# Depthwise taps of 20 middle rows moved to VectorE in a fused conv, attention and FFN kernel

## The chip, the cores and the metric

The kernel runs on one core of a Trainium2 chip. The metric is the device time of one launch in microseconds; 64 images go through in one launch.

## The reference

Two layers on x of shape (64, 96, 56, 56), cut to what matters here:

```python
# layer 0: expand, shift, shuffle, depthwise 3x3, gate, project, residual
out = silu(bn(einsum('bchw,oc->bohw', x, expand_w)))          # 96 -> 192 channels
out = channel_shuffle(shift_groups(out), groups=4)
dw  = bn(conv3x3_depthwise(out, dw_w))                        # 192 channels, padding 1
out = silu(bn(dw + bn(out * id_w)))
se  = relu(grouped_1x1(mean(out, (2, 3)), se_red_w, se_red_b))
se  = sigmoid(grouped_1x1(se, se_exp_w, se_exp_b))
x   = silu(bn(einsum('bchw,oc->bohw', out * se, proj_w)) + x)
# layer 1 on tokens t (b, 3136, 96)
h = relu(bn(layernorm(t) @ w1.T))                             # 192 wide
X = fft(h, axis=1);  y = ifft(relu(X.real*r - X.imag*i + rb) + 1j*relu(X.imag*r + X.real*i + ib)).real
t = t + bn(y @ w2.T)
t = t + q(q(relu(q(q8(layernorm(t)) @ q8(W1).T + b1))) @ q8(W2).T + b2)   # fp8 (e5m2) products
```

## The kernel before

Each image passes through a chain of small steps, each a Python function on one engine. `STEPS` lists them; `PLAN` gives each step instance a planned time, and the loop at the end issues the steps of all 64 images in the order of `b * PERIOD + PLAN[step][i]`. The numbers are used for nothing else: they only set the order in which each engine's queue gets its instructions, so that several images overlap. An engine works its queue in that order. Names end in what they do: `_mm` on TensorE; `ea_ev`, `eb_ev`, `dw_ev`, `ls`, `se1_ev`, `se2_th`, `pj_ev`, `c_sq`, `n_sq`, `sp_ev`, `f1_ev`, `f2_u`, `f2_r`, `w2_ev`, `i1_ev`, `x_ev`, `h_ev`, `h_q`, `o_ev` on ScalarE; `lt`, `se2_ev`, `se2_pw`, `pj_add`, `c_v`, `n_v`, `sp_v`, `w1_ev`, `f2_s`, `f2_p`, `i2_ev`, `n_x`, `h_b`, `o_b` on VectorE; `c_pow`, `n_pow`, `o_f` on GpSimd (POOL); the loads `x_in` and stores `o_st` on SyncE's (SP) queue.

The chain of one image: `ea` and `eb` expand (128 channels into `e_a`, L383; the other 64, in two half images, into `e_b`, L400). `dw` (L446) computes the 3x3 taps of the first 128 channels on TensorE as 32x32 diagonal matmuls, 16 tiles at a time, in two passes of 28 rows (4 strips of `PJ` = 7 rows, 392 columns each); `dw_ev` (L456) applies SiLU and sums for the gate. `lt` (L466, L468) computes the 9 taps of the other 64 channels on VectorE, one multiply and eight multiply-adds on 128 x 1568; `ls` (L471) is their SiLU. `se1`, `se2` compute the gate, `se2_pw` folds it into the projection weights, `pj` (L532, L537) projects, `pj_add` adds x and `pj_ev` (L549) writes the tokens. `c` and `sp` are the first layer norm, `w1` (L626, L638), `f1` (L653, L665), `f2` (L680, L690, L705 to L734), `w2` (L745, L757), `i1` (L786) and `i2` (L808) the spectral layer, `n` and `x` the second layer norm, `h` and `o` the FFN.

PSUM has two pools. `psa` is two double banks used in turn by `w1`, `f1`, `f2`, `w2`, `i1`, `i2`: each of these matmul steps waits until the user before last is read out (for `f2` by `f2_u` and `f2_s`). `psb` is four single banks for everything else; a `dw` pass and a `pj` half take all four at once. Every fp32 matmul appears in the trace as two instructions with a weight load each.

The set-up ahead of the loop loads the weights and tables, folds the batch norms on VectorE, and computes one product on TensorE (`ps_w1c`, L300), which stands ahead of all steps in TensorE's queue.

Of the kernel before, what the change touches and what calls it, by code (L numbers as in the profile page):

```python
# [7 lines left out]
F32 = mybir.dt.float32  # L8
# [3 lines left out]
ALU = mybir.AluOpType  # L12
# [17 lines left out]
PJ = 7  # L30
NG = 5
# [10 lines left out]
PERIOD = 116.056  # L42
PLAN = {
    "x_in": (-142.751, -132.334, -138.890, -139.641, -151.208, -133.652, -137.370),
    "ea_mm": (-127.116, -124.446, -119.920, -94.498, -104.745, -112.167, -106.964),
    "ea_ev": (-125.252, -124.279, -119.721, -94.105, -94.974, -110.456, -105.960),
    "eb_mm": (-110.852, -109.364, -102.468, -94.672, -100.705),
    "eb_ev": (-109.889, -108.508, -98.175, -94.671, -100.704),
    "dw_mm": (-77.186, -75.415, -71.686, -59.708, -58.836, -58.630),
    "dw_ev": (-67.184, -68.088, -65.354, -62.005, -53.949, -53.481, -53.376, -53.432),  # L50
    "lt": (-93.236, -91.843, -90.397, -86.333, -83.176, -78.618, -75.060, -71.072, -58.358),
    "ls": (-56.957,),
    "se1_mm": (-52.674,),
    "se1_ev": (-52.590,),
    "se2_mm": (-49.560,),
    "se2_ev": (-47.764,),
    "se2_th": (-46.882,),
    "se2_pw": (-44.842,),
    "pj_mm": (-44.604, -44.263, -36.259, -33.499),
    "pj_add": (-41.623, -41.337, -40.573, -40.255, -32.468, -30.814, -32.509, -32.127),  # L60
    "pj_ev": (-41.036, -40.637, -40.429, -36.736, -30.334, -29.230, -31.146, -29.797),
    "c_mm": (-24.403, -20.404, -19.123, -17.297, -18.726, -9.644, -8.872),
    "c_sq": (-23.198, -19.663, -17.391, -16.366, -11.963, -8.651, -8.871),
    "c_v": (-21.831, -17.939, -17.390, -11.021, -10.842, -8.366, -8.657),
    "c_pow": (-19.058, -12.292, -10.931, -8.952, -1.526, -3.948, -1.526),
    "sp_v": (-8.951, -1.525),
    "sp_mm": (-6.057, 0.802),
    "sp_ev": (-5.461, 1.113),
    "w1_mm": (1.423, -2.619, 3.588, 18.203, 8.943, 12.171, 13.999, 16.535),
    "w1_ev": (3.273, -0.045, 7.600, 20.920, 11.591, 14.999, 15.957, 19.212),  # L70
    "f1_mm": (21.608, 26.248, 24.638, 31.810, 32.559, 32.004),
    "f1_ev": (25.169, 25.895, 30.841, 28.844, 27.556, 26.595, 32.009, 32.411, 36.910, 36.732, 36.699, 35.929),
    "f2_mm": (37.220, 36.994, 44.528, 54.196, 60.721, 63.959),
    "f2_u": (39.991, 41.910, 38.664, 38.665, 56.185, 56.316, 56.071, 58.643, 62.858, 62.962, 66.464, 67.055),
    "f2_s": (42.369, 43.646, 41.684, 42.524, 58.496, 59.412, 59.011, 59.603, 66.349, 66.780, 67.365, 69.133),
    "f2_r": (44.699, 46.227, 59.499, 60.966, 71.228, 72.985),
    "f2_p": (46.153, 47.154, 60.124, 60.967, 72.402, 74.345),
    "w2_mm": (70.359, 71.061, 73.352, 79.154),
    "w2_ev": (70.421, 73.788, 79.483, 82.773),
    "i1_mm": (82.811, 83.639, 91.924),  # L80
    "i1_ev": (86.931, 93.317, 99.344),
    "i2_mm": (102.107, 101.737, 110.644, 111.766),
    "i2_ev": (106.004, 107.037, 104.651, 104.395, 113.248, 110.645, 115.503, 113.393),
    "n_mm": (109.042, 108.523, 116.336, 120.505, 126.604, 126.539, 137.374),
    "n_sq": (109.105, 109.021, 116.337, 120.506, 127.174, 126.540, 137.375),
    "n_v": (109.642, 109.022, 116.338, 120.507, 127.975, 126.902, 138.122),
    "n_pow": (110.809, 110.170, 116.496, 122.658, 132.126, 129.135, 139.318),
    "n_x": (112.520, 110.693, 119.248, 123.053, 133.298, 130.929, 139.362),
    "x_mm": (113.125, 114.113, 121.321, 126.216, 135.244, 138.382, 142.002),
    "x_ev": (114.896, 115.709, 126.025, 126.217, 137.926, 142.365, 142.302),  # L90
    "h_mm": (
        144.408, 144.539, 142.955, 151.653, 146.123, 151.741, 165.593, 167.081, 167.021, 179.037, 181.701, 184.163,
        183.315, 191.401, 194.122, 202.572, 203.025, 214.978, 205.482, 214.132, 209.133,
    ),
    "h_ev": (
        146.457, 147.163, 146.728, 153.132, 153.156, 154.262, 168.465, 171.753, 169.119, 180.037, 185.733, 184.280,
        187.040, 192.972, 195.243, 203.531, 205.107, 216.376, 208.878, 222.205, 212.052,
    ),
    "h_b": (
        146.899, 148.834, 148.614, 154.505, 157.941, 159.836, 170.515, 176.287, 174.097, 185.812, 187.639, 185.918,  # L100
        191.781, 195.030, 198.861, 204.123, 206.545, 220.428, 209.152, 226.370, 218.475,
    ),
    "h_q": (
        149.384, 151.139, 150.029, 159.215, 163.340, 163.159, 172.257, 183.329, 182.397, 187.024, 188.763, 189.403,
        196.328, 198.478, 200.406, 208.755, 210.002, 221.499, 217.314, 229.791, 224.579,
    ),
    "o_mm": (153.028, 179.101, 192.712, 203.850, 207.474, 223.800, 230.382),
    "o_ev": (154.015, 179.621, 193.552, 207.958, 209.955, 223.824, 232.254),
    "o_b": (167.276, 193.254, 201.506, 209.696, 210.604, 235.187, 237.499),
    "o_f": (171.766, 199.519, 206.356, 219.602, 231.322, 259.139, 253.186),  # L110
    "o_st": (197.792, 218.616, 214.282, 229.895, 257.122, 313.688, 263.438),
# [4 lines left out]
def conv_attn_ffn(  # L116
# [30 lines left out]
    tab_sel: bass.AP,  # L147
# [21 lines left out]
    nc.sync.dma_start(out=xi[GAP : GAP + 1].rearrange("p a b -> p (a b)"), in_=tab_ones)  # L169
# [17 lines left out]
    mid = load(mid_par, [128, 2, 22], "mid")  # L187
    mid_g = load(mid_grp, [128, NG, 12], "mid_g")
# [7 lines left out]
    eye = load(tab_eye, [CP, CP], "eye")  # L196
    sel = load(tab_sel, [CP, 2, 128], "sel")
# [10 lines left out]
    l_tab = load(tab_l, [128, NK, CP], "l_tab", nc.scalar)  # L208
    inv_tab = load(tab_inv, [CP, 2, HW], "inv_tab", nc.scalar)
    r_tab = load(tab_r, [128, HW, HW], "r_tab", nc.scalar)  # L210

    eps = const.tile([128, 1], F32, name="eps")
    nc.vector.memset(eps, 1e-5)
    mhalf = const.tile([128, NJ], F32, name="mhalf")
    nc.vector.memset(mhalf, -0.5)
# [35 lines left out]
    eyes = load(tab_eyes, [128, 32], "eyes")  # L251
# [7 lines left out]

    def row_fold(src, n, rows, name):  # L260

        b = work.tile([128, 4, n], F32, tag="ue", name=name + "_p")
        nc.gpsimd.dma_start(out=b[0:rows], in_=src.rearrange("(o f) c -> o f c", o=1).to_broadcast([rows, 4, n]))
        s = work.tile([128, 2, n], F32, tag="s", name=name)
        s = s[0:rows]
        nc.scalar.activation(s[:, 0], b[0:rows, 3, :], AF.Sqrt, bias=eps[0:rows])
        nc.vector.reciprocal(s[:, 0], s[:, 0])
        nc.vector.tensor_tensor(s[:, 0], s[:, 0], b[0:rows, 0, :], ALU.mult)
        nc.vector.tensor_tensor(s[:, 1], b[0:rows, 2, :], s[:, 0], ALU.mult)
        nc.vector.tensor_tensor(s[:, 1], b[0:rows, 1, :], s[:, 1], ALU.subtract)  # L270
# [7 lines left out]
    for e in range(2):  # L280
        nc.vector.tensor_copy(
            ex_b[:, e, :, e, :], ex_w[:, 128:MID].rearrange("p (u e i) -> p u e i", u=2, e=2)[:, :, e, :]
        )
# [26 lines left out]
    nc.vector.tensor_copy(eye8, eye, saturate=False)  # L310
# [16 lines left out]

    e_a = const.tile([128, PAD, PAD], F32, name="e_a")  # L330
    nc.gpsimd.memset(e_a, 0.0)
    e_b = const.tile([128, HH + 2, PAD], F32, name="e_b")
    nc.gpsimd.memset(e_b, 0.0)
    for i in range(NT):
        nc.vector.memset(t_buf[i], 0.0)

    buf_h = const.tile([128, C * HW + 8], F32, name="buf_h")
    nc.vector.memset(buf_h, 0.0)
    h_v = buf_h[:, 0 : C * HW].rearrange("p (c b) -> p c b", b=HW)
    pq_a = buf_h[:, 0 : NK * CP].rearrange("p (k f) -> p k f", f=CP)  # L340
    pq_b = buf_h[:, NK * CP : (NK + NS) * CP].rearrange("p (k f) -> p k f", f=CP)
    p_v = buf_h[:, 0 : 48 * HW].rearrange("p (b o) -> p b o", o=48)

    buf_g = const.tile([128, NK * MID], F32, name="buf_g")
    nc.vector.memset(buf_g, 0.0)
    g_v = buf_g.rearrange("p (k c) -> p k c", c=MID)
    u_v = buf_g[0:CP, 0 : C * 32].rearrange("p (o k) -> p o k", k=32)
    rs_full = const.tile([128, 2, NJ], F32, name="rs_full")
    nc.vector.memset(rs_full, 0.0)


# [24 lines left out]
    def x_in(b, i):  # L376
        load_x(b, i)
# [726 lines left out]
```

## Time and profile before

| what | value |
|---|---|
| median of 3 runs | 7462.52 us (7462.07 to 7469.69) |
| the profiled execution's own time | 7463.64 us |
| its span (first to last instruction) | 7461.9 us |
| granted TensorE clock, mean | 0.991 |
| busy: PE, PEld, DVE, ACT, POOL | 96%, 70%, 65%, 62%, 20% |
| first matmul of an `ea` step / of `f1` | 44.2 us / 130.16 us |
| last image's first `f1` matmul | 7332.96 us |

The page gives each engine's busy time (PE is TensorE, PEld its weight loads, DVE VectorE, ACT ScalarE), the chain of waits that ended last, and groups of instructions by source line: count after the x, then busy us, mean ns of one, idle time before it and what ended that. The ends of matmuls are modelled, so PE's busy share is not its efficiency.

### The profile page before, as it was taken

To read this page: it belongs to the slowest core of one execution; us is meant where nothing else is said; L and a number is where in the kernel's file an instruction comes from. 1 tells how busy PE (TensorE), PEld (TensorE's weight loads), DVE (VectorE), ACT (ScalarE), POOL (GpSimd) and SP (SyncE) were. 2 spreads that over 40 slices of the span, in tenths; PEclk is the share of its full clock that TensorE was granted. 3 is DMA by queue.
4 is the path that set the end of the run, shared out by engine and by line. 5 is a ranking of instruction groups with operands and counts; after the bars stand their busy time and mean duration, and the time that the engine had idled before them with its cause. 6 is when DMAs were issued, how large, how long until landed. Compare 5 with 4: busy or idle time off the path is not lost.

```text
span 7461.9 us, 383252 instructions
## 1 busy us (share of the span) xinstructions
PE 7176.9 (96%) x177666; PEld 5259.2 (70%) x177666; DVE 4829.5 (65%) x8795; ACT 4654.4 (62%) x9806; POOL 1513.6 (20%) x1360
## 2 busy tenths in 40 slices
PE   7999999999999999999999999999999999999997
PEld 4777777777777776777777777777777777777775
DVE  5666666666666666666666666666666666666664
ACT  3566666666665666656656666666566566665665
POOL 0221212212212122122121221221212212212112
PEclk9999999999999999999999999999999999999998
DMA  1010110110101101101011011010110110101100
GB/s 48 20 27 18 29 27 19 29 24 21 28 17 29 27 19 28 24 22 28 17 29 27 19 28 25 22 28 18 29 27 19 29 26 20 29 21 26 28 20 21
DMA packets 424331, 185.32 MB, mean 25 GB/s; under 512 B 378785, under 2 KB 422041, under 8 KB 422473
## 3 DMA queue, kind: packets, MB, share of 16 engines
q1 hardware_dynamic: 420970, 155.82, 9.1%
q8 instruction: 1392, 22.81, 1.3%
q10 hardware_dynamic: 1264, 3.48, 0.1%
q14 instruction: 209, 1.71, 0.1%
q0 software_dynamic: 496, 1.50, 0.1%
HBM read 82.80 MB, written 77.07 MB: 21 GB/s over the span
## 4 chain that ended last, share of the span: by engine, by line
PE 85%; ACT 6%; DVE 6%; issue 3%; DMA 0%; POOL 0%; POOLq 0%; SPq 0%; ACTq 0%
PE psa L653 9%; PE psa L626 9%; PE ps_d L446 8%; PE ps_eb L400 5%; PE ps_ea L383 5%; PE psa L808 5%; PE ps_pj L532 5%; PE ps_c L557 5%; PE psa L745 5%; PE ps_n L557 5%; PE psa L786 5%; PE psa L680 4%; PE ps_h L865 4%; PE ps_o L887 3%; DVE s L721 3%
## 5 line engine op out<-in xcount | busy, mean ns | idle before, releaser
L903 POOL TENSOR_TENSOR o<-t,o 112x448 f32<-112x448 f32 x448 | 613.9, 1370 | 3694.7 <-DMA out_dram<-o 1710.0
L446 PE MATMUL ps_d<-e_a,diag 32*32 32x392 f32 x36864 | 1033.2, 498 | 0.7 <-ACT d L456 0.7
L468 DVE SCALAR_TENSOR_TENSOR d_last<-e_b,taps,d_last 128x1568 f32<-128x1568 f32 x512 | 971.5, 1898 | 7.1
L875 DVE TENSOR_SCALAR y<-y,qb 128x448 f16<-128x448 f16 x1344 | 479.8, 365 | 683.9 <-ACT y L870 676.7
L568 DVE TENSOR_REDUCE v<-sq 112x4 f32<-112x384 f32 x896 | 491.3, 548 | 662.7 <-ACT sq L564 662.1
L446 PEld LDWEIGHTS ps_d<-e_a,diag 32*32 32x32 f32 x36864 | 673.6, 103 | 288.9 <-issue 40.0
L870 ACT CAST y<-ps_h 128x448 f16<-128x448 f32 x1344 | 697.2, 540 | 213.1 <-PE ps_h L865 209.5
L837 POOL TENSOR_TENSOR rs<-v,mhalf 112x4 f32<-112x4 f32 x448 | 490.3, 1099 | 1453.9 <-DVE v L569 1453.9
L881 ACT CAST h<-y 128x448 fp8e5<-128x448 f16 x1344 | 739.0, 571 | 3.0 <-DVE y L875 3.0
L653 PEld LDWEIGHTS psa<-f_tab,buf_h 128*56 128x56 f32 x24576 | 655.4, 131 | 77.8 <-DVE v L569 42.5
L626 PEld LDWEIGHTS psa<-w1c,t 112*64 112x64 f32 x14336 | 604.0, 137 | 141.4 <-DVE v L569 45.4
L653 PE MATMUL psa<-f_tab,buf_h 128*56 128x58 f32 x24576 | 688.9, 216 | 0.0
L626 PE MATMUL psa<-w1c,t 112*64 112x96 f32 x14336 | 676.2, 249 | 2.9 <-DMA t<-dev_t 1.4
L586 POOL TENSOR_TENSOR rs<-v,mhalf 112x4 f32<-112x4 f32 x448 | 447.6, 1012 | 763.6 <-DVE v L569 763.5
L638 DVE SCALAR_TENSOR_TENSOR buf_h<-psa,rs_full 128x768 f32<-128x768 f32 (+1 forms) x512 | 435.4, 851 | 137.4 <-PE psa L626 129.5
L543 DVE TENSOR_TENSOR ps_pj<-ps_pj,x 112x392 f32<-112x392 f32 x512 | 260.6, 566 | 404.5 <-PE ps_pj L537 392.3
L728 ACT ACTIVATE s<-s 128x896 f32<-128x896 f32 (+2 forms) x384 | 334.4, 887 | 288.8 <-DVE s L721 288.8
L388 ACT ACTIVATE e_a<-ps_ea 128x448 f32<-128x448 f32 x448 | 244.9, 547 | 412.5 <-PE ps_ea L383 412.5
L564 ACT ACTIVATE sq<-ps_n 112x384 f32<-112x384 f32 x448 | 214.1, 495 | 436.1 <-PE ps_n L557 434.8
L734 DVE SCALAR_TENSOR_TENSOR buf_h<-ue,s 128x448 f32<-128x448 f32 (+2 forms) x768 | 406.8, 580 | 109.4 <-ACT s L728 109.4
L549 ACT ACTIVATE t<-ps_pj,pjbn_b 112x392 f32<-112x392 f32 x512 | 281.4, 620 | 284.5 <-DVE ps_pj L543 284.5
L786 PE MATMUL psa<-inv_tab,buf_g 112*32 112x56 f32 x24576 | 350.5, 214 | 110.5 <-issue 108.8
(175 smaller groups left out, 13024.5 us busy)
## 6 DMA issues: line engine op xcount, KB each, us to landing
x<-in_x SPq DMA_DIRECT2D x896, 84.0 KB, 3.2
out_dram<-o SPq DMA_DIRECT2D x896, 84.0 KB, 2.2
l_tab<-in_tab_l ACTq DMA_DIRECT2D x1, 1624.0 KB
r_tab<-in_tab_r ACTq DMA_DIRECT2D x1, 1568.0 KB
t<-dev_t SPq DMA_DIRECT2D x64, 7.0 KB, 2.1
t<-dev_t SPq DMA_DIRECT2D x64, 5.2 KB
ex_row_p<-in_expand_row POOLq DMA_DIRECT2D x1, 336.0 KB, 4.5
s_p<-in_bn POOLq DMA_DIRECT2D x1, 288.0 KB, 3.8
```

The lines of the kernel that those rows point to most:

```text
L446: nc.tensor.matmul(pss[r][j * 32 : j * 32 + 32], lhsT=diag[pr, tap, :], rhs=e_a[pr, r0 : r0 + PJ, dx : dx + HW], start=tap == 0, stop=tap ...
L468: nc.vector.scalar_tensor_tensor(d_last, win, w, d_last, ALU.mult, ALU.add)
L557: nc.tensor.matmul(cen[c0:c1, k, 0:C], lhsT=t_of(b)[:, n0 + c0 : n0 + c1], rhs=center, start=True, stop=True)
L568: nc.vector.tensor_reduce(v, sq, AX.X, ALU.add)
L626: nc.tensor.matmul(ps[hc * 64 : hc * 64 + 64, k, 0:C], lhsT=t[:, n0 : n0 + 64], rhs=w1c[:, hc * C : hc * C + C], start=True, stop=True,)
L653: nc.tensor.matmul(ps[r * 64 : r * 64 + HW, k, 0 : 2 * NK], lhsT=buf_h[:, n0 : n0 + HW], rhs=f_tab[:, r, :], start=True, stop=True,)
L786: nc.tensor.matmul(ps[p0 : p0 + 32, k, 0:HW], lhsT=u_v[:, oh * 48 + o, :], rhs=inv_tab[:, r, :], start=True, stop=True,)
L837: nc.gpsimd.tensor_tensor(rs, held.pop(("nv", b, g)), mhalf[0:CP, 0:4], ALU.pow)
L870: nc.scalar.copy(y16, held.pop(("h", b, i)))
L875: nc.vector.tensor_scalar(y16, y16, qb1[:, i % 3 : i % 3 + 1], 0.0, ALU.add, ALU.max)
L881: nc.scalar.copy(held["h8", b, j][:, m, :], held.pop(("y", b, i)), saturate=False)
L903: nc.gpsimd.tensor_tensor(o32, rows, o16, ALU.add)
```

## The change

The middle 20 rows (18 to 37) of the first 128 channels are taken from TensorE: `mt` computes their nine taps on VectorE from `e_a` into `d_mid` (128 x 1120), with `ms` as their SiLU and sum on ScalarE. The other 36 rows (9 + 9 at the top, 9 + 9 at the bottom) go through `dw` in one pass with strips of `PJ` = 9 rows, 504 columns. The projection of the middle rows is one matmul of 128 channels and 5 rows (280 columns) per strip in place of four of 32 channels. The gate has 6 sums instead of 9. `sp_mm` selects with four half-width matmuls from the identity table in place of two with `tab_sel`, which is gone. In the set-up, x of the first image is loaded right after `ex_w`, `ex_w` is folded first, `mid`, `mid_g` and `eyes` are loaded by ScalarE's queue, and `l_tab` and `r_tab` come last on SP. All times of `PLAN` and `PERIOD` are new (those of the steps named below are shown).

```diff
-PJ = 7
-NG = 5
+PJ = 9
+M0 = 2 * PJ
+MR = HW - 4 * PJ
+MJ = MR // 4
+NG = 6
-PERIOD = 116.056
+PERIOD = 140.265
...
-    "dw_mm": (-77.186, -75.415, -71.686, -59.708, -58.836, -58.630),
+    "dw_mm": (-112.745, -112.718, -112.047),
-    "lt": (-93.236, -91.843, -90.397, -86.333, -83.176, -78.618, -75.060, -71.072, -58.358),
+    "lt": (-136.700, -135.995, -135.558, -134.088, -134.025, -130.160, -122.585, -110.579, -107.986),
+    "mt": (-164.940, -164.052, -163.371, -149.054, -134.393, -134.063, -132.364, -119.142, -113.460),
+    "ms": (-111.901,),
-    "se1_mm": (-52.674,),
+    "se1_mm": (-94.074,),
-    "pj_mm": (-44.604, -44.263, -36.259, -33.499),
+    "pj_mm": (-69.552, -69.551, -65.748, -61.381),
-    "w1_ev": (3.273, -0.045, 7.600, 20.920, 11.591, 14.999, 15.957, 19.212),
+    "w1_ev": (-1.771, -19.170, -8.762, -4.229, -10.279, -4.199, -8.276, -1.831),
-    "f1_mm": (21.608, 26.248, 24.638, 31.810, 32.559, 32.004),
+    "f1_mm": (9.106, 8.289, 6.986, 1.458, 9.457, 8.749),
-    "f2_mm": (37.220, 36.994, 44.528, 54.196, 60.721, 63.959),
+    "f2_mm": (11.234, 10.157, 22.124, 26.950, 29.584, 36.004),
-    "f2_s": (42.369, 43.646, 41.684, 42.524, 58.496, 59.412, 59.011, 59.603, 66.349, 66.780, 67.365, 69.133),
+    "f2_s": (13.743, 13.743, 12.484, 12.496, 26.842, 26.842, 27.498, 31.087, 34.039, 34.367, 47.926, 51.650),
-    "w2_mm": (70.359, 71.061, 73.352, 79.154),
+    "w2_mm": (57.877, 50.003, 70.914, 73.115),
...
+    for i in range(NCH):
+        load_x(0, i)
...
     def x_in(b, i):
-        load_x(b, i)
+        if b > 0:
+            load_x(b, i)
...
-    d_buf = const.tile([128, 2, 4, PJ, HW], F32, name="d")
+    d_buf = const.tile([128, 4, PJ, HW], F32, name="d")
+    d_mid = const.tile([128, MR, HW], F32, name="d_mid")
...
+    def start_row(n):
+        i, j = divmod(n, 4)
+        if i == 0:
+            return j % 2 * (M0 + MR) + j // 2 * PJ, PJ
+        return M0 + (j % 2 * 2 + j // 2) * MJ, MJ
...
-    def dw_mm(b, n):
-        i, third = divmod(n, 3)
+    def dw_mm(b, third):
...
+    def one_tap(d, e, h, r0, n):
         tap = (4, 0, 1, 2, 3, 5, 6, 7, 8)[n]
         dy, dx = divmod(tap, 3)
+        win = e[:, r0 + dy : r0 + dy + d.shape[1], dx : dx + HW]
+        w = taps[:, h, tap : tap + 1]
         if n == 0:
+            nc.vector.tensor_scalar(d, win, w, None, ALU.mult)
         else:
+            nc.vector.scalar_tensor_tensor(d, win, w, d, ALU.mult, ALU.add)
+    def lt(b, n):
+        one_tap(d_last, e_b, 1, 0, n)
...
+    def mt(b, n):
+        one_tap(d_mid, e_a, 0, M0, n)
+    def ms(b, i):
+        nc.scalar.activation(d_mid, d_mid, AF.Silu, bias=mid_b[:, 5:6], accum_out=sums_of(b)[:, 5:6])
...
+        elif part == 0:
             for j in range(4):
+                r0, n = start_row(4 + j)
+                nc.tensor.matmul(
+                    pss[j], lhsT=pw[:, 5, :], rhs=d_mid[:, r0 - M0 : r0 - M0 + n, :], start=True, stop=False
+                )
```

Sorted, the new `PLAN` puts these steps on VectorE from one `w1_ev0` on, while TensorE has `f1` and `f2` of the same image b (the taps are those of image b + 1): `n_x4, n_x6, lt0, lt1, lt2, mt4, lt3, mt5, lt4, mt6, h_b3, lt5, h_b0, f2_s2, f2_s3, h_b4, f2_s0, f2_s1, h_b5, lt6, o_b5, mt7, h_b2, f2_p1, h_b1, f2_p0, o_b6, mt8, f2_s4, f2_s5, f2_s6, f2_p2, lt7, f2_s7, lt8, f2_p3, f2_s8, f2_s9`. `mt0` to `mt3` come before it, among `n_v`, `n_x`, `i2_ev` and `w1_ev`. TensorE's order there is `f1_mm3, 2, 1, 5, 0, 4`, `f2_mm1, f2_mm0, f2_mm2, f2_mm3, dw_mm0` to `2`, `f2_mm4, f2_mm5, se1_mm, w2_mm1, se2_mm, w2_mm0, pj_mm0`, with x, o, h and ea products between.

## The prediction

> **What bounds the kernel now.** I read the page's busy shares first, then its chain:
>
> ```profile
> PE 7176.9 (96%) x177666; PEld 5259.2 (70%) x177666; DVE 4829.5 (65%) x8795; ACT 4654.4 (62%) x9806; POOL 1513.6 (20%) x1360
> ...
> PE 85%; ACT 6%; DVE 6%; issue 3%; DMA 0%; POOL 0%; POOLq 0%; SPq 0%; ACTq 0%
> ```
>
> TensorE sets the end, VectorE and ScalarE have a third of the span free. But these are averages over stages. The groups of the work that changes:
>
> ```profile
> L446 PE MATMUL ps_d<-e_a,diag 32*32 32x392 f32 x36864 | 1033.2, 498 | 0.7 <-ACT d L456 0.7
> L468 DVE SCALAR_TENSOR_TENSOR d_last<-e_b,taps,d_last 128x1568 f32<-128x1568 f32 x512 | 971.5, 1898 | 7.1
> ```
>
> The taps of the first 128 channels cost TensorE 1033.2/64 = 16.1 us an image; the other 64 channels' taps cost VectorE 15.2 us plus one multiply of 1.04. Then I cut one image's period into stages with the windows view (from f1 of one image to f1 of the next, so two to three images are in flight in each). Columns: stretch, length, busy us of PE, PEld, DVE, ACT, POOL, clock:
>
> ```profile
> 2989.60:3028.00 38.40, 38.40 (x1144) 30.06 (x1140) 34.33 (x44) 30.06 (x63) 3.38 (x3) 1.00 0.02 4
> 3028.00:3036.50 8.50, 7.67 (x210) 6.34 (x209) 5.77 (x14) 7.34 (x18) 0.00 (x0) 1.00 0.01 4
> 3036.50:3050.10 13.60, 13.60 (x195) 8.04 (x192) 4.98 (x12) 8.91 (x18) 1.30 (x1) 1.00 0.23 53
> 3050.10:3065.40 15.30, 13.22 (x478) 10.37 (x476) 6.13 (x17) 9.85 (x19) 4.82 (x5) 0.89 0.38 84
> 3065.40:3105.00 39.60, 39.60 (x769) 27.44 (x768) 23.68 (x51) 16.41 (x40) 13.98 (x14) 1.00 0.06 16
> ```
>
> This table carries the prediction. Row 1 (f1, f2 and both `dw` passes, up to `se1_mm`) has VectorE busy 34.33 of 38.40 us: no 65% there, but 89%. Row 5 has it at 60%. Where the new taps fall decides what they cost.
>
> In the timeline, what TensorE and VectorE do back to back:
>
> ```profile
> 3005.84 7.95 PE L446 MATMUL ps_d<-e_a,diag 32*32 32x392 f32 x288
> ...
> 3050.09 2.86 PE L786 MATMUL psa<-inv_tab,buf_g 112*32 112x56 f32 x216
> 3055.03 1.00 PE L786 MATMUL psa<-inv_tab,buf_g 112*32 112x56 f32 x40 [2.08 <-issue]
> ```
> ```profile
> 3126.71 0.33 DVE L875 TENSOR_SCALAR y<-y,qb 128x448 f16<-128x448 f16 x1
> 3126.96 1.84 DVE L468 SCALAR_TENSOR_TENSOR d_last<-e_b,taps,d_last 128x1568 f32<-128x1568 f32 x1
> 3128.72 2.22 DVE L734 SCALAR_TENSOR_TENSOR buf_h<-ue,s 128x448 f32<-128x448 f32 x4
> ```
>
> One pass of 9 taps takes 7.9 us. A VectorE instruction's successor starts about 0.08 us before its end (3126.96 + 1.84 against 3128.72), so I count start to start. The first `f1` starts at 130.16 and the last at 7332.96: 63 periods of **114.33 us**. Span = 130.2 + 63 x 114.33 + 128.9 = 7461.9; the execution's own time is 7463.64, 1.7 more, and the median of the runs shown is 7462.52, 1.1 below it.
>
> **The Trainium skill.** "PSUM — Partial Sum Buffer", Specifications (TRN2): a bank holds 512 fp32 values, so 9 rows x 56 = 504 just fit; the trace has 392. "VectorE: DVE Perf Modes", Mode 1× (REGULAR): fp32 with a second tensor runs at one result a cycle, 0.96 GHz; 1568 elements are 1.63 us, the trace shows 1.84 to 1.90. "SBUF — State Buffer", Who interferes with whom: a VectorE instruction with two SBUF inputs collides with a GpSimd one that reads SBUF. The taps' median is 1.850, their mean 1.898, their maximum 2.277, which agrees. The `mt` taps are of that kind.
>
> **The change, part by part, per image.**
>
> *TensorE, taps.* 288 of 576 matmuls go; the others grow from 392 to 504 columns. A group of 16 tiles now takes 7.9/18 = 0.439 us. A long row shows what a column costs: `ea` (448 columns) and `eb` (392) spend 0.445 and 0.363 us per matmul step, at most 0.83 ns a column; so 0.439 + 112 x 0.83 = 0.532, x18 = **9.6 us** (8.0 if nothing grows, 10.2 in proportion). Two passes back to back take 15.9: 6.3 saved. What hides the new pass is below: `f2_mm4` behind it waits for `f2_s5` on VectorE anyway, so 8.0 or 10.2 instead of 9.6 moves nothing; without that cover they are worth -1.6 or +0.6.
>
> *TensorE, projection.* Columns: before 2 x (4 x 392 + 2 x 392) per row group; after 6 x 504 + (4 + 2) x 280: both 4704. The full-height matmuls of 280 columns run one at a time, those of 32 rows four at a time, which the count includes. Nothing; bounds -0.5 to +1 us.
>
> *TensorE, gate and selector.* `se1` loses 3 of 9 matmuls (x2 instructions x 34 ns = -0.2), `se2` gains one, `sp_mm` has 4 half-width matmuls for 2 (0 to +0.5). Nothing.
>
> *ScalarE.* Eight `dw_ev` of 0.78 (0.586 + 0.203 for the sum) become four of about 0.92 and one `ms` of 1.4: -1.2 us. Not the bound.
>
> *VectorE.* Added: `mt`, one multiply (1.04 x 20/28 = 0.74) and eight taps of 1120 elements. Start to start a `lt` tap takes 1.76 undisturbed and 1.82 on average; by size 1.26, by the page's cycle for the 448 elements that are missing 1.35; I take 1.30. Sum **11.1 us**. `mt0` to `mt3` lie in the last stage (row 5), under TensorE: nothing. `mt4` to `mt8` lie between `f1` and `se1`: 6.5 us in row 1's stage.
>
> *That stage after the change.* The order says what VectorE does there, in one unbroken run from `w1_ev0`, which `f1_mm3` waits for, to `f2_s9`, which frees the PSUM buffer of `w2_mm1`: nine `lt` (1.0 + 8 x 1.82 = 15.6), five `mt` (6.5), eight `f2_s` of 448 (pairs, 1.31 each: 10.5), two of 392 (1.21: 2.4), four `f2_p` (1.07: 4.3), six `h_b` and two `o_b` (0.25: 2.0), two `n_x` (0.47: 0.9). **42.2 us.** TensorE's own work there, `f1_mm3` to `f2_mm5`: 38.4 - 6.3 and some 3.5 of x, o and ea products that the new order has there, about 36. I looked for each of these VectorE steps whether its ScalarE input is there in time (`f2_u`, `f2_r`, `h_ev` in that queue's order): it is, so VectorE runs through. The stage goes from 38.4 to 42.2: it gives back the whole saving and 3.8 more. The waits that this adds: TensorE stands before `f2_mm2` and `f2_mm3` (PSUM held until `f2_s3`, `f2_s1`) with `dw` queued behind, and before `w2_mm1` with the gate behind; ScalarE's `ms` waits for `mt8`, with `f2_r2` and all `dw_ev` queued behind, and the h products wait for the banks that these free. All of it lies inside the 42.2, since VectorE meanwhile has work.
>
> *Then the gate.* `se1_mm` waits for `ls` and `o_ev0`; `w2_mm1` for `f2_s9`. ScalarE has queued in front of `h_ev12`, whose bank `pj_mm0` needs: 9.6 us of `ls`, `o_ev`, `f2_u`, `f2_r4`, four `h_q`, four `h_ev`; it gets there 7.4 us after `f2_s9` (8.5 now, row 2).
>
> *Then TensorE alone,* from `pj_mm0` to the next `w1_ev0`: rows 3 to 5 take 68.5 us now, of which my sum of single steps explains 65.1; the other 3.4 are mostly the wait of 2.08 for instructions and its clock of 0.89. The new order's steps there add up to 62.9 (the products that moved into the first stage are missing). There the `i1` steps are apart, with slower matmuls between them, so I keep a third of that wait: **64.0** (62.9 to 66.3).
>
> Period: 42.2 + 7.4 + 64.0 = **113.6**, against 114.33.
>
> *Start.* The first `ea` starts at 44.2 us, after `ps_w1c` at 43.3, which VectorE's fold of w1 releases behind memsets of 2.7 to 4.7 us each. The new order loads x and folds ex_w first, but the w1c product stays ahead in TensorE's queue: -10 us (0 to -25). Moved DMAs: SP issues x at 0.78 us each (11 in 8.56), so the constants behind them come 11 us later; l_tab and r_tab, last on SP now, are wanted after 120 us. Three small loads go to ScalarE's queue. x_in of later images stays where SP has gaps (3058 to 3074). The first image's taps take 27 us of VectorE beside 10 of TensorE, for 19 of TensorE now: the first image gives some of the start back, in the -10.
>
> Sum: 7461.9 + 63 x (113.6 - 114.33) - 10 = 7406; + 1.7 - 1.1: **7405 us**. Break-even is a period of 114.5, or a VectorE stage of 43.1.
>
> **Rivals.**
>
> *VectorE's stage is longer (slower).* If the taps and products cost their listed means without overlap (`lt` 1.90, `mt` 1.39, `f2_s` 1.37, `f2_p` 1.23), the stage is 45.5 us, the period 116.9, the time 7461.9 + 63 x 2.57 - 10 + 0.6 = **7615**. For it: collisions with POOL's sums, five more taps exposed to them. Against: start-to-start times in the timeline. It decides from 43.1 us on; any wait of TensorE on POOL's or ScalarE's short chains adds the same way.
>
> *The saving arrives whole.* TensorE stays the bound: 114.33 - 6.3 = 108.0, **7057**. Row 1's 34.33 + 6.5 speaks against it: VectorE can't fit into 32.
>
> *No difference.* Stage and waits cancel within 0.2% (about what a measurement of this kernel can tell from no change), 7448 to 7477; the shift of 0.77% is small beside the terms.
>
> *The loads first do nothing,* because ps_w1c holds TensorE: +10 on the forecast, inside its range.
>
> **How the numbers follow.** Forecast (small gain) 0.47, its own range 7240 to 7447: low end with mt at 1.26 and no wait for instructions, a period of 111. Whole saving 0.05, no difference 0.09, slower 0.39. Faster 0.52, same 0.09, slower 0.39. Both signs are likely, so the range is 7240 to 7640.
>
> **What would show it.** Right: TensorE's busy share falls to some 92 to 93%, VectorE's rises to 74%; in row 1's stage VectorE is over 95% busy and TensorE waits for VectorE's `s`, `ue` (f2_s) at f2 and w2; `dw` has one pass of about 9.6 us; `mt` taps of 1.35 listed; the stage is 41 to 43.5 us. Wrong: a stage under 39 us with TensorE full; or TensorE waiting in row 5's stage; or a first `ea` still at 44 us.

## The result and the profile after

The kernel after the change takes 7642.35 us (median of 4 runs, 7634.26 to 7651.36) beside 7465.10 us of the kernel before on the same chip (7462.07 to 7469.69): a ratio of **1.0237 (95% interval 1.0219 to 1.0255), slower by 2.4%**. The forecast was 7405 us with a range to 7640. The profiled execution has a span of 7632.3 us.

The page after: busy shares, the shares of the chain that ended last, and three groups (busy us in total, mean ns of one).

```profile
PE 6957.4 (91%) x157954; PEld 5111.4 (67%) x157954; DVE 5425.0 (71%) x9367; ACT 4640.9 (61%) x9422; POOL 1763.2 (23%) x1366
...
PE 62%; DVE 26%; issue 6%; ACT 3%; POOL 3%; DMA 0%; POOLq 0%; SPq 0%; ACTq 0%; DVEq 0%
...
L478 DVE SCALAR_TENSOR_TENSOR d_last<-e_b,taps,d_last 128x1568 f32<-128x1568 f32 x512 | 945.5, 1847 | 9.7
...
L478 DVE SCALAR_TENSOR_TENSOR d_mid<-e_a,taps,d_mid 128x1120 f32<-128x1120 f32 x512 | 705.7, 1378 | 4.6
...
L457 PE MATMUL ps_d<-e_a,diag 32*32 32x504 f32 x18432 | 617.0, 590 | 0.0
```

The operations cost what the forecast said: the one `dw` pass is 617.0/64 = 9.64 us of TensorE (16.1 before), a middle tap 1.378 us listed. VectorE's part of the chain that ended last went from 6% to 26%. Yet TensorE's busy time fell by only 219.5 us, although 6.5 us x 64 = 416 us of `dw` went. Something made its other work longer.

The period is cut as before, now for the image whose `f1` starts at 3403.80: `f1` to `se1` (VectorE's stage below), `se1` to `pj_mm0` (the gate), `pj_mm0` to the next `f1` (the last part); then four stretches around the border of the first two. Columns of the windows view: stretch, length, busy us of PE, PEld, DVE, ACT, POOL, granted TensorE clock, DMA share, GB/s.

```profile
3403.80:3445.74 41.94, 36.73 (x887) 27.40 (x887) 41.27 (x51) 31.54 (x63) 6.98 (x3) 0.98 0.06 15
3445.74:3454.98 9.24, 8.55 (x180) 7.40 (x180) 5.34 (x14) 6.88 (x16) 0.00 (x0) 0.71 0.02 4
3454.98:3521.07 66.09, 62.41 (x1406) 44.24 (x1401) 37.44 (x83) 33.85 (x71) 20.22 (x19) 1.00 0.14 32
3440.55:3443.16 2.61, 0.01 (x2) 0.00 (x0) 2.57 (x3) 1.99 (x4) 0.00 (x0) 1.00 0.00 0
3443.16:3444.32 1.16, 1.16 (x19) 0.89 (x20) 1.16 (x3) 1.11 (x2) 0.00 (x0) 1.00 0.03 7
3444.32:3451.15 6.83, 5.66 (x85) 4.55 (x79) 5.46 (x13) 5.09 (x11) 0.00 (x0) 0.50 0.01 2
3451.15:3454.98 3.83, 3.83 (x112) 3.06 (x104) 1.27 (x3) 3.21 (x8) 0.00 (x0) 1.00 0.02 4
```

Row 1 is the stage that the forecast put on VectorE: 41.27 of 41.94 us busy. Row 4 is TensorE idle for 2.61 us in it. Row 6 is new: 1.2 us after TensorE has resumed, its **granted clock falls to one half for 6.83 us**. The timeline shows what that does (start, length, idle before it and who ended it):

```profile
3439.15 1.40 PE L923 MATMUL ps_o<-h,q 128*112 128x448 fp8e5 x6
3443.16 0.35 PE L901 MATMUL ps_h<-xq,q 96*128 96x448 fp8e5 x1 [2.60 <-ACT y L906]
...
3447.07 2.82 PE L781 MATMUL psa<-w2a,buf_h 128*64 128x96 f32 x32 [0.68 <-DVE ue L760]
...
3452.72 1.53 PE L781 MATMUL psa<-w2a,buf_h 128*64 128x96 f32 x32
```

The same 32 `w2` matmuls take 2.82 us at half clock and 1.53 at full. The idle ahead of `h_mm10` waits for a PSUM bank that ScalarE's `h_ev6` frees; `h_ev6` stands behind `f2_r3`, and that waits for VectorE:

```profile
3441.17 0.95 ACT L764 ACTIVATE s<-s 128x896 f32<-128x896 f32 x1 [0.82 <-DVE s L757]
3442.02 0.66 ACT L741 ACTIVATE ue<-psa,fb 128x392 f32<-128x392 f32 x1
3442.59 0.95 ACT L906 CAST y<-ps_h 128x448 f16<-128x448 f32 x2
```

The waits view (us in total, times, longest) has three waits that the kernel before does not have in its list:

```profile
DVE d_mid L476 <- ACT e_a L396: 327.3, 63, 5.2
...
PE ps_n L586 <- DVE xt L879: 84.8, 62, 1.4
...
PE psa L662 <- DVE t L857: 37.2, 62, 0.6
```

In VectorE's timeline the first one stands where `mt0` heads the queue:

```profile
3377.08 0.56 DVE L879 TENSOR_TENSOR xt<-ps_n,rs 112x384 fp8e5<-112x384 f32 x1 [1.04 <-POOL rs L873]
3382.86 0.81 DVE L476 TENSOR_SCALAR d_mid<-e_a,taps 128x1120 f32<-128x1120 f32 x1 [5.22 <-ACT e_a L396]
3383.70 2.81 DVE L478 SCALAR_TENSOR_TENSOR d_mid<-e_a,taps,d_mid 128x1120 f32<-128x1120 f32 x2
3386.43 0.33 DVE L911 TENSOR_SCALAR y<-y,qb 128x448 f16<-128x448 f16 x1
3386.67 1.16 DVE L857 SCALAR_TENSOR_TENSOR t<-psa,bn2c_b,t 112x392 f32<-112x392 f32 x2
```

VectorE stands 5.22 us for `ea` of group 2, and then three taps run while `h_b16`, `i2_ev7`, `i2_ev6` (L857) and the norm steps wait behind them.

The means over all 63 periods, from the starts of `f1`, `se1` and `pj_mm0` and the records of the granted clock in each trace. Half clock is the time that the trace records at a granted clock of one half. All periods below are read in this way; the last of the 63 is shorter in every trace, since no further image follows.

| kernel | f1 to se1 | se1 to pj_mm0 | pj_mm0 to f1 | period | half clock per period |
|---|---|---|---|---|---|
| before | 38.56 | 8.41 | 67.36 | 114.33 | 0.92 |
| after | 41.90 | 9.48 | 65.87 | 117.25 | 8.67 |

The span adds up: first `f1` at 118.6 + 63 x 117.25 + 126.8 behind the last = 7632.

### The profile page after: what moved, and what is told of

Its sections match the earlier page's. It is cut to its first block, busy times and chain, and to the rows that moved or that the text cites. A ratio compares the mean times of both kernels' runs of the same rounds, so it can differ in the third digit from the quotient of the medians.

```text
span 7632.3 us, 343376 instructions
## 1 busy us (share of the span) xinstructions
PE 6957.4 (91%) x157954; PEld 5111.4 (67%) x157954; DVE 5425.0 (71%) x9367; ACT 4640.9 (61%) x9422; POOL 1763.2 (23%) x1366
## 4 chain that ended last, share of the span: by engine, by line
PE 62%; DVE 26%; issue 6%; ACT 3%; POOL 3%; DMA 0%; POOLq 0%; SPq 0%; ACTq 0%; DVEq 0%
PE psa L689 9%; PE psa L662 6%; PE psa L781 6%; DVE s L757 5%; PE psa L844 5%; DVE ue L760 4%; DVE d_mid L478 4%; PE psa L822 4%; PE ps_c L586 4%; PE ps_eb L408 4%; DVE buf_h L770 4%; PE ps_pj L554 3%; PE psa L793 3%; PE ps_n L586 3%; POOL rs L873 3%
## 5 line engine op out<-in xcount | busy, mean ns | idle before, releaser
L939 POOL TENSOR_TENSOR o<-t,o 112x448 f32<-112x448 f32 x448 | 834.8, 1869 | 3582.3 <-DVE o L933 2463.7
L478 DVE SCALAR_TENSOR_TENSOR d_mid<-e_a,taps,d_mid 128x1120 f32<-128x1120 f32 x512 | 705.7, 1378 | 4.6
L662 PEld LDWEIGHTS psa<-w1c,t 112*64 112x64 f32 x14336 | 611.3, 137 | 99.4 <-DVE t L857 45.5
L572 DVE TENSOR_TENSOR ps_pj<-ps_pj,x 112x504 f32<-112x504 f32 (+1 forms) x512 | 261.6, 568 | 541.6 <-PE ps_pj L566 532.6
L457 PE MATMUL ps_d<-e_a,diag 32*32 32x504 f32 x18432 | 617.0, 590 | 0.0
L716 PEld LDWEIGHTS psa<-l_tab,buf_g 128*64 128x64 f32 x7424 | 387.4, 145 | 341.4 <-issue 157.7
L901 PE MATMUL ps_h<-xq,q 96*128 96x448 fp8e5 x1344 | 474.1, 377 | 152.4 <-ACT y L906 138.5
L895 ACT CAST xq<-ps_x 96x448 fp8e5<-96x448 f32 x448 | 236.0, 527 | 557.0 <-PE ps_x L888 557.0
L716 PE MATMUL psa<-l_tab,buf_g 128*64 128x112 f32 x7424 | 446.6, 275 | 114.8 <-DVE ue L760 113.2
L578 ACT ACTIVATE t<-ps_pj,pjbn_b 112x504 f32<-112x504 f32 (+1 forms) x512 | 279.6, 625 | 373.2 <-DVE ps_pj L572 364.6
L457 PEld LDWEIGHTS ps_d<-e_a,diag 32*32 32x32 f32 x18432 | 370.0, 103 | 199.6 <-issue 53.4
```

Of the source, the lines that this page charges most:

```text
L457: nc.tensor.matmul(pss[r][j * 32 : j * 32 + 32], lhsT=diag[pr, tap, :], rhs=e_a[pr, r0 : r0 + PJ, dx : dx + HW], start=tap == 0, stop=tap ...
L478: nc.vector.scalar_tensor_tensor(d, win, w, d, ALU.mult, ALU.add)
L662: nc.tensor.matmul(ps[hc * 64 : hc * 64 + 64, k, 0:C], lhsT=t[:, n0 : n0 + 64], rhs=w1c[:, hc * C : hc * C + C], start=True, stop=True,)
L716: nc.tensor.matmul(ps[c0 : c0 + 64, k, 0:CP], lhsT=g_v[:, k1, c0 : c0 + 64], rhs=l_tab[:, k1, :], start=True, stop=True,)
L939: nc.gpsimd.tensor_tensor(o32, rows, o16, ALU.add)
```

## The experiments

Theory 1 at the start: the gain was lost to the clock, which halves after the idle that VectorE's long stage leaves on TensorE. Its rivals: the gate has its own chain and the clock is a symptom; or VectorE's longer stage is the whole loss. All edits are to the kernel after the change, all ratios are to the kernel before on the same chip.

**Filling TensorE's idle.** The same sum is made five times over, so that only the idle goes.

```
-        for m in range(3):
+        for _ in range(5 if j == 0 else 1):
+            for m in range(3):
```

> The kernel after the change, with the three matmuls of o_mm of the first group made five times over (each repetition starts the sum anew, so the value is the same): 12 matmuls, some 2.6 us of TensorE work per image put into TensorE's idle stretch ahead of h_mm10; nothing else is moved. Theory 1 (the forecast lost its gain to TensorE's clock, which halves after that idle stretch and stays down for 7 to 17 us of every period): the clock stays at 1.00 through the period (half clock under 1.5 us per period, 8.7 before this edit), the VectorE-bound stage stays at 42, the gate returns to 7.4 to 8.0, the rest to 64 to 65; period about 113.5, time 7370 to 7450. Rival 1 (the gate's chain through ScalarE and VectorE sets its length and the clock is only a symptom): 7620 to 7660. Rival 2 (VectorE's longer stage is the whole loss): 7620 to 7660, and with the added TensorE work no gain anywhere.

7573.6 us, ratio 1.016 (1.0143 to 1.0177): by the two ratios some 57 us less than after, but above the 7370 to 7450 of theory 1. Period 116.19 (41.85 + 8.63 + 65.71), half clock 3.14 us. Two neighbouring periods of this trace, three rows each:

```profile
3375.65:3417.60 41.95, 38.65 (x899) 28.92 (x899) 41.29 (x51) 31.55 (x62) 7.14 (x3) 1.00 0.05 15
3417.60:3424.94 7.34, 6.31 (x180) 5.43 (x180) 5.50 (x14) 6.89 (x16) 0.00 (x0) 1.00 0.01 2
3424.94:3490.01 65.07, 62.07 (x1413) 44.06 (x1405) 37.40 (x82) 33.96 (x72) 20.13 (x19) 1.00 0.14 32
3490.01:3531.96 41.95, 38.49 (x899) 28.94 (x899) 41.29 (x51) 31.55 (x62) 7.13 (x3) 1.00 0.06 15
3531.96:3540.76 8.80, 7.77 (x179) 6.78 (x180) 5.50 (x14) 6.89 (x16) 0.00 (x0) 0.81 0.02 5
3540.76:3606.37 65.61, 62.03 (x1413) 44.15 (x1405) 37.41 (x82) 33.86 (x72) 20.13 (x19) 1.00 0.14 32
```

One kernel, one order: with the clock kept the gate is 7.34, the forecast's 7.4; with half clock in it 8.80. In the 22 of 63 periods without half clock the gate is 7.34 every time, and the parts are 41.94 + 7.34 + 65.75 = 115.03; in the 32 with 3.4 us of it the gate is 8.6 to 8.9. So the clock is real, but it is not all: the last part stays at 65.7, where the forecast had 64.0.

**One order on ScalarE.** `f2_r[3]` goes behind `h_ev6`, `h_ev7` and `f2_u9` (31.088 to 31.373).

> The kernel after the change, with f2_r[3] moved on ScalarE behind h_ev6, h_ev7 and f2_u9, so that h_mm10's bank comes free without waiting for VectorE's f2_s7. Theory 1 (an idle stretch of TensorE anywhere in the VectorE-bound stage halves the clock; the stage has some 36 us of TensorE work in 42): the idle stretch of 2.6 us ahead of h_mm10 goes and stands later instead, ahead of h_mm9, se1 or w2_mm1; the clock still halves for 7 us or more per period, time 7590 to 7650. Rival (that one order on ScalarE is the cause): no long idle, clock 1.00, 7390 to 7480.

7648.34 us, 1.0259 (1.0244 to 1.0275): no gain, as theory 1 said. TensorE's idle went elsewhere:

```profile
3566.18 0.64 PE L497 MATMUL ps_se<-sums,rd_w 128*24 128x1 f32 x12 [2.43 <-ACT o L928]
3567.50 2.82 PE L781 MATMUL psa<-w2a,buf_h 128*64 128x96 f32 x32 [0.68 <-DVE ue L760]
```

Now 2.43 us ahead of `se1`, and again `w2` at 2.82. The half clock is 6.72 us per period. A wait moved inside a stage that another engine sets only moves the idle.

**The taps out of VectorE's stage**, without and with the filling:

```
-    "ea_mm": (-166.379, -168.555, -167.472, -180.658, -173.715, -159.950, -127.809),
-    "ea_ev": (-164.984, -167.775, -166.091, -178.609, -172.105, -156.666, -124.805),
+    "ea_mm": (-166.379, -167.472, -168.555, -180.658, -173.715, -159.950, -127.809),
+    "ea_ev": (-164.984, -166.091, -167.775, -178.609, -172.105, -156.666, -124.805),
-    "mt": (-164.940, -164.052, -163.371, -149.054, -134.393, -134.063, -132.364, -119.142, -113.460),
+    "mt": (-165.930, -165.830, -164.930, -164.830, -164.530, -164.030, -158.930, -149.050, -148.530),
```

> The kernel after the change, with the middle rows' taps out of the VectorE-bound stage: ea_mm and ea_ev of groups 1 and 2 change places, mt0 to mt5 stand one after the other where VectorE waited 5.2 us for e_a, mt6 to mt8 among the w1_ev of the last stage; VectorE's work between f1 and f2_s9 falls by five taps of 1.30, from 42.0 to about 35.5. Theory 1: that stage becomes TensorE's own, 36.5 to 38.5; no idle over 1 us is left in it, the clock stays at 1.00 (half clock under 2 us per period), gate 7.4 to 8.5, the rest 64 to 66.5; period 109 to 112, time 7110 to 7300. Rival 1 (the gate's length comes from its ScalarE and VectorE chain whatever the clock): gate stays at 9.5 to 11, period 112.5 to 114, 7330 to 7430. Rival 2 (VectorE's taps only come to stand ahead of w1_ev in the last stage): the rest grows by 5 or more, 7500 to 7650.

> The taps moved as in the run before and the o_mm of the first group made five times over as in the first. Theory 1: if the moved taps leave no idle that drops the clock, the added 2.6 us of TensorE work lie on the path: 100 to 165 us slower than with the moved taps alone. If the clock still drops there, the filling gains up to 150 us instead. Rival 1 and rival 2: as with the moved taps alone, plus or minus 20.

7743.62 us (1.0383, 1.0367 to 1.0398) and 7556.95 us (1.0134, 1.0119 to 1.0150). Theory 1 expected 7110 to 7300 for the first and failed; rivals 1 and 2 gave lower times too. Three things came together. VectorE's stage only fell from 41.9 to 40.6: three of the five taps were taken from in front of `h_b3`, where VectorE then stood for 3.4 us, and only two from behind it. The taps in the last part held the norm steps back. TensorE's idle ahead of `n_mm` grew from 1.37 to 2.36 us, here in the run with the filling:

```profile
3587.03 0.88 PE L586 MATMUL ps_n<-center,t 112*64 112x96 f32 x16 [2.36 <-DVE xt L879]
3587.74 2.30 PE L662 MATMUL psa<-w1c,t 112*64 112x96 f32 x32
```

After this idle too the clock halved (a record of one half begins at 3588.24): 32 `w1` matmuls take 2.30 us, for 1.54 at full clock in the kernel after. Half clock without filling 11.49 us per period, the most of all runs; with it 3.63. Filling that costs TensorE 2.3 us per image (18 matmuls in 3.67 us instead of 6 in 1.40) made this kernel 187 us faster, more than the up to 150 expected. In the periods of the second run without half clock the last part is 66.2 (10 periods, the last one left out); in those with 3.4 or 6.8 us of it 68.4 and 70.2.

**Filling more, and the place of mt0's wait.** To the filling above come two more, in `se1_mm` and in `h_mm`, as below. The second kernel adds the exchange of `ea` groups 1 and 2 alone, the taps where the change put them.

```
-        for g in range(NG):
+        for n in range(3 * NG):
+            g = n % NG
...
+        for _ in range(4 if i == 9 else 1):
```

> The kernel after the change with three fillings of TensorE's idle in the VectorE-bound stage (values unchanged): o_mm of the first group five times over, h_mm9 four times, se1's accumulation three times, some 4.5 us of TensorE work per image. In the run that filled only ahead of h_mm10, the 22 of 63 periods without half clock took 41.9 + 7.3 + 65.8 = 115.0 us, the others more. Theory 1, sharpened (two terms were mis-sized: the clock, worth about 2.2 us per period, and TensorE's last stage, 65.8 for 64.0 even at full clock): half clock under 1.5 us per period, period 115.0 to 115.6, time 7480 to 7540; so slower than the kernel before still. Rival (the clock is the whole miss): 7400 to 7430. Rival (the gate's own chain; filling delays se1): 7570 or more.

> As the run before, and besides ea_mm and ea_ev of groups 1 and 2 change places, so that mt0, which stands at the head of VectorE's queue and waited 5.2 us for e_a of group 2 with h_b16, i2_ev7, i2_ev6, n_v3 and n_v2 queued behind it, can start about 3.5 us earlier. Theory 1, sharpened (the 1.8 us too much of the last stage come from that wait: VectorE's later n_v and n_x hold TensorE at n_mm and w1): TensorE's wait for xt at n_mm (1.37 us) and for t at w1 (0.60) shrink to under 1.0 together, the last stage falls to 64.0 to 64.8, time 60 to 110 us below the run before (7390 to 7460). Rival (the last stage is TensorE's own work): no change within 20 us.

7545.91 us (1.0088, 1.0071 to 1.0105) and 7393.69 us (**0.9888**, 0.9866 to 0.9910). The first came 6 us above its range: half clock 2.28 us, not under 1.5; its 31 periods without half clock took 115.05. The exchange alone is worth 152 us, more than expected: the last part fell from 65.76 to 63.56 (139 us over 63 periods), and the waits of TensorE for `xt` at `n_mm` and for `t` at `w1` are gone from the list. This is the second loss.

**The exchange alone**, no filling:

> The kernel after the change with only ea_mm and ea_ev of groups 1 and 2 exchanged: no filling, the taps where they were. Theory 1 (two separate losses: mt0's wait for e_a, worth 2.3 us per period in the last stage, and the clock after TensorE's idle in the VectorE-bound stage): the last stage falls from 65.9 to 63.5 to 64.2, the half clock of about 7 to 9 us per period stays; stage 41.9, gate 8.5 to 9.8; period 114.3 to 115.5, time 7450 to 7530, within 1% of the kernel before. Rival (the half clock came from the idle of the last stage too and goes with it): 7390 to 7420, as with the filling.

7511.92 us, 1.0070 (1.0048 to 1.0092), as theory 1 said, with the gate and the half clock a little above its ranges: 41.94 + 9.96 + 63.49, half clock 9.81 us. A period of it:

```profile
3468.29:3510.24 41.95, 37.59 (x887) 28.18 (x887) 41.29 (x51) 31.56 (x63) 7.04 (x3) 0.97 0.06 15
3510.24:3521.69 11.45, 10.69 (x180) 9.09 (x180) 6.80 (x19) 7.64 (x17) 0.00 (x0) 0.53 0.01 2
3521.69:3585.59 63.90, 62.26 (x1409) 44.36 (x1401) 36.39 (x79) 33.20 (x70) 20.25 (x19) 1.00 0.15 33
```

The last part is healed, the gate at a clock of 0.53 is not: two separate losses.

**Filling with wide matmuls.** The half clock that the more filled runs kept began mostly 1.0 to 2.7 us after the start of `se1`, whose matmuls have one column. So `h_mm9` (448 columns) runs five times ahead of `se1` and three times behind it, and `se1` once; `o_mm` of the first group stays at five times, and the exchange is in.

> As the run with the exchange of ea groups 1 and 2 and the filling (o_mm of the first group five times over), but the filling around se1 is of wide matmuls: h_mm9 five times ahead of se1 and three times more behind it (448 columns, values unchanged), se1's accumulation of one column only once. In the run before it 45 of 63 periods had no half clock and took 112.8 us, the 18 others 113.5 to 117.9; where it fell, it began at se1's 1-column matmuls after an idle of 0.76 us. Theory 1 (the clock is kept by work that fills the array, not by many small instructions): half clock under 0.7 us per period (1.41 in that run), period 112.7 to 113.1, time 7345 to 7385, gate 7.3 to 7.6. Rival (the rest of the half clock has another cause): 1.4 us of it remain, 7385 to 7405. Rival (the added matmuls now delay w2_mm1): 7410 or more.

7364.37 us, **0.9835 (0.9822 to 0.9849)**: the fastest of all, as theory 1 said. The gate's TensorE lines and one period of it:

```profile
3433.01 1.12 PE L907 MATMUL ps_h<-xq,q 96*128 96x448 fp8e5 x5
3434.71 0.46 PE L497 MATMUL ps_se<-sums,rd_w 128*24 128x1 f32 x12 [0.58 <-ACT o L935]
3435.10 0.74 PE L502 MATMUL ps_h<-xq,q 96*128 96x448 fp8e5 x3
3436.03 1.53 PE L786 MATMUL psa<-w2a,buf_h 128*64 128x96 f32 x32 [0.19 <-DVE ue L765]
```
```profile
3392.64:3434.59 41.95, 39.26 (x903) 29.26 (x903) 41.29 (x51) 31.54 (x63) 7.07 (x3) 1.00 0.06 16
3434.59:3441.93 7.34, 7.03 (x183) 5.69 (x183) 5.46 (x14) 6.88 (x17) 0.00 (x0) 1.00 0.01 2
3441.93:3504.78 62.85, 61.74 (x1413) 44.03 (x1402) 37.73 (x83) 33.91 (x72) 20.19 (x19) 1.00 0.15 33
```

In 62 of 63 periods there is no half clock; the period is 112.92. Over the runs with VectorE's stage unchanged (among them the one with the first image's loads late, below), the stretch from `f1` to `pj_mm0` follows the half clock that falls into the gate:

| run | half clock per period | of it in the gate | f1 to pj_mm0 |
|---|---|---|---|
| exchange alone | 9.81 | 7.21 | 51.90 |
| loads late | 9.59 | 6.83 | 51.77 |
| one order on ScalarE | 6.72 | 6.34 | 51.70 |
| after | 8.67 | 6.05 | 51.38 |
| filling | 3.14 | 3.09 | 50.48 |
| filling more | 2.28 | 2.05 | 50.12 |
| exchange, filling more | 1.41 | 1.26 | 49.79 |
| exchange, wide filling | 0.11 | 0.11 | 49.28 |

Half clock in VectorE's stage adds little: the one order on ScalarE has 1.95 us per period less than after in all, 0.29 more in the gate, and is the longer of the two.

**A shorter stage for VectorE.** Twice I tried to gain what moving the taps had not, with the exchange of `ea` groups 1 and 2 in all three kernels. First `mt4` to `mt8` singly in gaps of the last part and `lt5`, `lt6` ahead of `h_b3`; then also `lt7`, `lt8`, `ls` and `f2_s8` earlier, without and with filling.

```
-    "lt": (-136.700, -135.995, -135.558, -134.088, -134.025, -130.160, -122.585, -110.579, -107.986),
+    "lt": (-136.700, -135.995, -135.558, -134.088, -134.025, -130.365, -130.315, -110.579, -107.986),
-    "mt": (-164.940, -164.052, -163.371, -149.054, -134.393, -134.063, -132.364, -119.142, -113.460),
+    "mt": (-165.930, -165.830, -164.930, -164.830, -158.930, -154.030, -153.030, -149.050, -148.630),
```

and in the other two, from this one on:

```
-    "lt": (-136.700, -135.995, -135.558, -134.088, -134.025, -130.365, -130.315, -110.579, -107.986),
-    "ls": (-107.985,),
+    "lt": (-136.700, -135.995, -135.558, -134.088, -134.025, -130.365, -130.315, -130.065, -114.265),
+    "ls": (-111.0125,),
...
-    "f2_p": (25.614, 23.503, 29.485, 33.211, 70.171, 61.080),
+    "f2_p": (25.614, 23.503, 29.485, 34.100, 70.171, 61.080),
```

> No filling. The kernel after the change with the middle taps mt0 to mt3 in VectorE's wait for e_a (groups 1 and 2 of ea exchanged), mt4 to mt8 singly in VectorE's gaps among n_x and w1_ev, and the last channels' taps lt5 and lt6 moved ahead of h_b3, where VectorE stood idle for 3.4 us in the run with the moved taps. Behind h_b3 VectorE then has about 24.7 us of work instead of 31 (28.3 in the run with the moved taps). Theory 1, sharpened (the first stage is 12.6 us until h_b3 can start, then VectorE's work behind it): stage 37.5 to 39, gate 7.1 to 8.5, the rest 64.5 to 67; with no idle over 2 us the half clock is under 3 us per period; period 110 to 113, time 7190 to 7380: faster than both. Rival 1 (the stage has another bound at 40.7, as in the run with the moved taps): 7450 to 7560. Rival 2 (the idle pieces that remain halve the clock as before): 7500 to 7650.

> No filling. As in the run with the taps spread, and besides lt7 directly behind h_b0 (VectorE stood 1.9 us there), lt8 ahead of f2_s4 (1.0 us), ls on ScalarE ahead of dw_ev0 (2.7 us idle) instead of behind the f2_u9, f2_s8 ahead of f2_p3. Theory 1 (in that run the first stage was held at 40.7 not by VectorE's work but by the dw pass, which starts 23.4 us after f1 and ends at 33, and ScalarE's 8.3 us behind it, 1.9 of them ls): stage 38.5 to 39.5, gate 6.5 to 8.5, the rest 65 to 66; period 110.5 to 113.5, time 7210 to 7400. Rival (VectorE's f2_s and f2_p behind dw hold the stage): 40.5, 7450 to 7490, as in that run. Rival (the idle pieces that remain halve the clock): 7400 to 7480.

> As the run before, with o_mm of the first group three times over and h_mm9 three times (1.9 us of TensorE work per image, values unchanged). Theory 1: the half clock falls under 2 us per period; 20 to 130 us below the run before, 7180 to 7300. Rival (no idle is left there to fill): the added work costs up to 120 us.

7476.44 us (0.9996, 0.9986 to 1.0006), 7533.01 us (1.0090, 1.0075 to 1.0105) and 7475.58 us (1.0010, 1.0001 to 1.0018): all above what theory 1 expected, although the filling again took 57 us off, with 2.33 us of half clock left. In the first the stage stayed at 40.65, as its rival 1 said, with VectorE busy for only 36.18 of 40.70 us:

```profile
3453.16:3493.86 40.70, 36.38 (x888) 27.41 (x887) 36.18 (x47) 31.37 (x62) 5.04 (x4) 1.00 0.06 17
```

So VectorE is no longer what sets it. In the second, `se1` came earlier (39.53), and the wait went on to `w2_mm1`:

```profile
3519.05 0.63 DVE L757 SCALAR_TENSOR_TENSOR s<-psa,fb,ue 128x392 f32<-128x392 f32 x1 [5.05 <-ACT ue L741]
```
```profile
3522.66 2.20 PE L781 MATMUL psa<-w2a,buf_h 128*64 128x96 f32 x32 [2.46 <-DVE ue L760]
```

VectorE's last `f2_s` of that stage now wait for ScalarE's `f2_u8`, which is queued behind the `dw_ev`: the stage then runs dw, ScalarE, VectorE, TensorE in a row, and again with an idle of over 2 us that costs clock (5.47 us at half per period). How far this chain can be shortened stays open.

**The first image's loads** issued behind the constants again.

```
-    for i in range(NCH):
-        load_x(0, i)
...
-        if b > 0:
-            load_x(b, i)
+        load_x(b, i)
```

> The kernel after the change, with the loads of the first image issued behind the constants again, not ahead of them; all else as after the change. The forecast gave the earlier loads 10 us: first ea at 40 to 50 instead of 29.3, first f1 about 10 us later, time 5 to 15 us above the kernel after. Rival (they do nothing, since ps_w1c or the fold of ex_w holds TensorE): within 3 us.

7671.06 us, 1.0255 (1.0237 to 1.0272). The first `ea` starts at 40.2 instead of 29.3, the first `f1` 11.8 us later (130.4 for 118.6). The intervals of the two ratios overlap, so the whole time alone does not show the 10 us; the trace's start does.

## Why the prediction was wrong

**Right.** The operations: `dw` 9.6 (9.64), a tap 1.30 start to start (3409.40 to 3410.70 in the trace). The `dw` figure is in part luck: 0.445 us for 448 columns and 0.363 for 392 are 0.99 and 0.93 ns a column, not at most 0.83, and would have given some 9.8 to 9.9; 9.64 measured makes it 0.86. The VectorE-bound stage, busy without a gap, and that it gives back the saving of 6.3 us: 42.2 forecast to `f2_s9`, 41.9 measured to `se1`; taken together with the gate, so that the border does not matter, 49.6 forecast and 49.3 measured wherever the clock holds. TensorE's waits for VectorE at f2 and w2. The start: -10 forecast, -11.8 measured by undoing it. Within the slower rival the sign was right and the mechanism was not: no stage of 45.5 exists; VectorE runs at start-to-start times, as I had argued against that rival. That its 7615 lies near 7642 is luck.

**Wrong, first step: "it gets there 7.4 us after `f2_s9`".** The gate's queue was read correctly, the TensorE steps in it were priced at full clock. I had put the roughly 5 us of idle that VectorE's stage leaves on TensorE (41.94 - 36.73) at nothing beyond the stage itself. It has a second price: 8.67 us of half clock per period, mostly in the gate. `f1` to `pj_mm0` is 51.38 for 49.6: 1.8 x 63 = 112 us. Removing the half clock by filling brings 49.28. The row with clock 0.89 in the profile before, and my own 3.4 us for it and an issue wait, were the hint.

**Wrong, second step: "`mt0` to `mt3` lie in the last stage (row 5), under TensorE: nothing".** Their 4.7 us of work do lie there; their wait does not. `mt0` needs `e_a` of group 2, which TensorE makes late, and stands at the head of VectorE's queue for 5.22 us. I had asked what waits for the middle taps in the first stage and not in the last. The last part is 65.87 for 64.0: 1.9 x 63 = 118 us. The exchange of two `ea` groups brings 63.5. I had the warning sign in the list (TensorE waiting in row 5's stage) and not in the sum.

**The sum.** 112 + 118 = 230 of the 237 us between 7405 and 7642; the execution from which the periods are read took 7634, 8 us less than the median. The forecast's own last line adds up to 7406.5 rather than 7405, which changes nothing. With both repaired, by the exchange and by filling that the forecast did not have, the kernel takes 7364 where the kernel before takes 7487: a ratio of 0.9835, for 0.992 forecast.

The Trainium skill, "TensorE: Matmul & The Clock Gate", Part 1, says that a hardware monitor halves TensorE's clock after an idle window of about 3.4 us, the window being free-running, 3413 ns long. The traces agree on the window: all 71 records of half clock after the change start on one grid of 3413.3 ns, to within 1 ns, and the usual one lasts 6.83 us, two times 3.413. If an idle window means one without any work, they disagree: 2.61 us of idle, or 2.36 or 2.43, were enough here (2.04 in most periods after the change), and in the filled runs 0.76 us ahead of one-column matmuls.

What fits all 14 traces is how busy TensorE is in each window of that grid. In the one that ends where the half clock above begins (3440.91 to 3444.32) it is busy for 1.16 of 3.41 us. Between the first and the last `f1`, and with the gate's one-column matmuls left out, the clock fell after all 296 full-clock windows that were less than 40% busy, after 384 of the 632 between 40% and 56%, and after none of the 27628 above; the busy shares are modelled ones. So the same wait can cost clock or not, by where it falls in the grid: the kernel before stands for 1.69 us on average ahead of `i1` in each image, and its clock fell in 17 of 63 periods.

## What to carry to other kernels

Work moved from the engine that bounds to another one leaves idle on the first; ask what that idle does to its clock, and look at the granted clock stretch by stretch, since a mean of 0.959 hides a gate at 0.71 (a mean of 0.954 one at 0.53, with the exchange alone). A moved step brings its wait along: write down what each first instruction of a moved group waits for, and what is queued behind it, in every stage where a part of it lands. If a stage can't be made dense, a few useless wide matmuls in the idle can cost less than the half clock that they prevent.

## What the runs showed that I had not expected

- Adding 2.3 us of TensorE work per image made the kernel some 57 us faster (ratio 1.0237 to 1.016), and 187 us in the kernel with the taps moved (7744 to 7557).
- In the period shown half clock began 1.2 us after the work had resumed (in the others from 1.2 us before that to 2.6 us after), so it can fall on innocent instructions: the idle ahead of `h_mm10` is paid for by `w2`.
- With the exchange, three rounds of one-column `se1` matmuls and four `h_mm9` left 1.41 us of half clock per period; one round and eight `h_mm9` of 448 columns left 0.11. That suggests that small matmuls count little for the clock; the two edits differ in more than that, so they do not show it alone. The windows counted above point the same way: with the one-column matmuls counted as work, 113 windows over 56% busy were followed by half clock, without them none.
- POOL's sums `o_f` went from a mean of 1370 ns before to 1869 ns; no wait of TensorE follows from it. The traces show where: before, the 61 taps that ran beside an `o_f` took 2.26 to 2.28 us and the other 451 at most 1.85, so the prediction was right to see a collision in their spread. After, the 122 `mt` taps beside an `o_f` take no longer than the others (1.37 and 1.38 us), and it is `o_f` that takes 3.02 us on average there and 1.44 elsewhere: the taps moved did not pay for it.
